# Softmax totals of attention for two groups of heads in one pass of the matmul array, and their inverses spread by transfers inside the chip

## The chip, the cores and the metric

The kernel runs on one core of one Trainium2 chip. A core has a matmul engine (TensorE, PE in the profile), a vector engine (VectorE, DVE), a scalar engine for activation functions (ScalarE, ACT), GpSimd (POOL) and SyncE (SP), from which most transfers are issued. Each engine works through its own queue in order, and waits on semaphores for what others make. Working data is in SBUF (128 partitions); matmuls write to PSUM, whose banks hold 512 float32 values on each of 128 partitions. The metric is device time in microseconds (us), from the start to the end of one execution; lower is better.

## The reference, cut to what matters

Four layers follow each other on x of shape (8, 512, 32, 32): an attention layer with an inner iteration (layer 0), a second attention (layer 1), a filtered leaky ReLU (layer 2), and convolutions with weights mixed per sample (layer 3). The change is in layer 0 alone:

```python
h = group_norm(x, gn_scale, gn_bias)
qkv = einsum('oc,bchw->bohw', qkv_w, h) + qkv_b       # 512 channels each for q, k, v
q, k, v = to_heads(q), to_heads(k), to_heads(v)       # 8 heads of 64, S = 1024 positions
attn = softmax(einsum('bnsd,bntd->bnst', q, k) * 64 ** -0.5, axis=-1)
h = einsum('bnst,bntd->bnsd', attn, v)
for _ in range(3):                                    # h is (B, S, 512) here
    h = h + 0.1 * tanh(einsum('bsc,oc->bso', h, inl_w) + inl_b)
x = x + einsum('oc,bchw->bohw', proj_w, h) + proj_b
```

The softmax's division is done last: the kernel multiplies exponentials by v, adds up the exponentials over the keys, and multiplies the product by one over that total.

## The kernel before, in words

All of it is float32. The eight samples ("batches", `b`) go through layers 0 to 2 one after another; layer 3 follows for all. The attention of layer 0 is in `layer0`. A batch has eight *groups* `g`, each one (oc, sh): oc is one of four pairs of heads (128 channels, a head on each 64 partitions) and sh one of two halves of 512 query positions. Groups 0 to 3 are the first half of the positions, 4 to 7 the second. A group has eight *steps*, one for each 128 keys, so a batch has 64 steps.

In each step `i` the loop records, in this order, `scores(i)`, `weighted(i - 2)` and whatever closes an earlier group:

- `scores` (L827) multiplies k by q in four matmuls of 64x64 tiles (two heads, two halves of the keys) that sit on the four quarters of the array; ScalarE takes the exponential of both banks in one instruction (L846); VectorE adds the result to the group's running sum `acc` (L850, L852, and L854 at the eighth step, which also records a sum for a later test of overflow). The exponentials have six buffers.
- `weighted` (L868) multiplies the exponentials by v, again four 64x64 tiles, into two banks `av` of the group. At the eighth step ScalarE copies one bank to `part` (L875) and VectorE adds the other to it (L876), which gives the group's columns of the output `hf`. Even groups take their two banks from one pool of PSUM, odd ones from another.
- `closing(g, at)` stands `at` steps after the step in which the sum of group g can be used. At 0, `totalled` adds up `acc` over the 128 partitions with a matrix of ones: two matmuls (L881) of 128 rows and 64 columns, one for each head, into the group's first `av` bank, so that every one of a head's 64 partitions gets the same total. VectorE takes the reciprocal of 512 columns in two instructions of 256 (L889), at 0 and 1; at 2 it multiplies `hf` by it (L894); at 5 ScalarE reads it once more for the overflow test (L898).

The order on TensorE, VectorE and ScalarE in this stage is the order in which the program records it (`tc.manual_schedule`). Elsewhere, and on SP and GpSimd, a scheduler orders the work and puts in the waits. The last group's closing stands inside the first product of the inner iteration (`within=last_total`, matmuls at L552), together with the sums of quarters of `hf` that this product needs (`T_hf`, L513).

Buffers: `big_tile` gives one of seven SBUF buffers of 16 KB per partition (x, q, k, v, hf, `T_hf` and others take turns in them); `tmp(..., HALF)` one of four of 2 KB (for `part` and `inv`); `sums` one of two of 4 KB (for `acc`). A new tile takes a free buffer, and its first write waits until that buffer's last reader is done. `x = load_x(b)` loads the batch's input again for the projection's sum; on SP's queue the load of the next query weights (L461) stands behind it. `layer2_constants` builds the filter matrices of layer 2 during batch 0, in a big buffer that GpSimd writes first.

Each matmul instruction leaves two records of matmul and two of weight load in the profile: L827 has 4096 records for 8 batches of 64 steps of four matmuls.

Of the kernel before, what the change touches and what calls it, by code (L numbers as in the profile page):

```python
# [17 lines left out]
P = 128  # L18
B, C, H, W = 8, 512, 32, 32
S = H * W  # L20
CC = C // P
SC = S // P
HALF = 512
NH = 8
HD = C // NH
# [12 lines left out]
WE = NE * WX  # L38
EARLY = B - 1
PARTS = ("A11", "A12", "-A22", "S1", "S2", "S3", "S4")  # L40


BOUND = 1e20
# [11 lines left out]
def tile_sequence(ctx: ExitStack, tc: tile.TileContext, a: dict, out: bass.AP, shifted: bool):  # L55
    nc = tc.nc
# [11 lines left out]
    def big_tile(name, shape):  # L68
        return big.tile(shape, F32, tag="big", name=name)
# [5 lines left out]
    def tmp(name, n=HALF):  # L75
        if n == HALF:
            return work.tile([P, n], F32, tag="half", name=name, bufs=4)
        return work.tile([P, n], F32, tag="tmp", name=name, bufs=6)

    def sums(name):  # L80
        return work.tile([P, S], F32, tag="sums", name=name, bufs=2)
# [26 lines left out]
    ones = const.tile([P, P], F32, name="ones")  # L108
# [453 lines left out]
    def all_of(gen):  # L562
        for _ in gen:
            pass
# [232 lines left out]
    def layer0(b, q, k, v, w):  # L797
        hf = big_tile(f"hf_{b}", [P, CC, S])
        rows = [slice(HD * r, HD * r + HD) for r in range(2)]
        shifts = None  # L800
        if shifted:
            shifts = big_tile(f"shifts_{b}", [P, CC, S])
            for oc in range(CC):
                for r in range(2):
                    row_shifts(
                        f"{b}_{oc}_{r}", [q[rows[r], oc, :]] * 2,
                        [k[rows[r], oc, ts(h, HALF)] for h in range(2)],
                        [shifts[HD * r : HD * r + 1, oc, :]],
                    )

        groups = [(oc, sh) for sh in range(2) for oc in range(CC)]
        exps, accs, avs, copies = {}, {}, {}, {}

        def scores(t):
            g, jc = divmod(t, SC)
            oc, sh = groups[g]
            apart = t == 1
            if apart:  # L820
                ps = [bank(ps_tp, f"scores_{b}_{t}_{r}") for r in range(2)]
            else:
                pair = ps_sc.tile([P, S], F32, tag="scores", name=f"scores_{b}_{t}")
                ps = [pair[:, ts(r, HALF)] for r in range(2)]
            for r in range(2):
                for c in range(2):
                    nc.tensor.matmul(  # L827
                        ps[r][rows[c]],
                        k[rows[r], oc, jc * P + c * HD : jc * P + c * HD + HD],
                        q[rows[r], oc, ts(sh, HALF)],  # L830
                        start=True, stop=(shifts is None),
                    )
            if shifts is not None:
                for r in range(2):
                    for c in range(2):
                        nc.tensor.matmul(
                            ps[r][rows[c]], ones[HD * r : HD * r + 1, 0:HD],
                            shifts[HD * r : HD * r + 1, oc, ts(sh, HALF)],
                            start=False, stop=True,
                        )  # L840
            e = tmp(f"e_{b}_{t}", S)
            if apart:
                for r in range(2):
                    nc.scalar.activation(e[:, ts(r, HALF)], ps[r], AF.Exp, scale=HD ** -0.5)
            else:
                nc.scalar.activation(e, pair, AF.Exp, scale=HD ** -0.5)  # L846
            exps[t] = e
            if jc == 1:
                accs[g] = sums(f"acc_{b}_{g}")
                nc.vector.tensor_add(accs[g], exps[t - 1], e)  # L850
            elif 1 < jc < SC - 1:
                nc.vector.tensor_add(accs[g], accs[g], e)  # L852
            elif jc == SC - 1:
                nc.vector.scalar_tensor_tensor(  # L854
                    accs[g], accs[g], 1.0, e, ALU.mult, ALU.add,
                    accum_out=seen_sums[:, b, g : g + 1],
                )

        def weighted(t):
            g, jc = divmod(t, SC)  # L860
            oc, sh = groups[g]
            e = exps.pop(t)
            if jc == 0:
                pool = (ps_mm, ps_tp)[g % 2]
                avs[g] = [bank(pool, f"av_{b}_{g}_{r}") for r in range(2)]
            for r in range(2):
                for c in range(2):
                    nc.tensor.matmul(  # L868
                        avs[g][r][rows[c]], v[rows[r], jc, ts(2 * oc + c, HD)],
                        e[rows[r], ts(c, HALF)],  # L870
                        start=(jc == 0), stop=(jc == SC - 1),
                    )
            if jc == SC - 1:
                part = tmp(f"part_{b}_{g}", HALF)
                nc.scalar.copy(part, avs[g][0])  # L875
                nc.vector.tensor_add(hf[:, oc, ts(sh, HALF)], avs[g][1], part)  # L876

        def totalled(g):
            acc, ps = accs.pop(g), avs.pop(g)[0]
            for r in range(2):  # L880
                nc.tensor.matmul(  # L881
                    ps[rows[r]], ones[:, 0:HD], acc[:, ts(r, HALF)], start=True, stop=True
                )
            totals[g] = ps
            copies[g] = tmp(f"inv_{b}_{g}", HALF)

        def inverse(g, part):
            at = ts(part, QR)
            nc.vector.reciprocal(copies[g][:, at], totals[g][:, at])  # L889

        def scaled(g):
            oc, sh = groups[g]
            dst = hf[:, oc, ts(sh, HALF)]
            nc.vector.tensor_mul(dst, dst, copies[g])  # L894

        def copied(g):
            inv = copies.pop(g)
            nc.scalar.activation(  # L898
                inv, inv, AF.Copy, accum_out=seen_sums[:, b, NG + g : NG + g + 1]
            )  # L900

        def closing(g, at):

            if at == 0:
                totalled(g)
                inverse(g, 0)
            elif at == 1:
                inverse(g, 1)
            elif at == 2:
                scaled(g)  # L910
            elif at == 5:
                copied(g)

        lag, steps, last_g = 2, len(groups) * SC, len(groups) - 1
        totals = {}
        engines = mybir.EngineType
        with tc.manual_schedule(engines={engines.PE, engines.DVE, engines.Activation}):
            for i in range(steps + lag):
                if i < steps:
                    scores(i)  # L920
                if i >= lag:
                    weighted(i - lag)
                g, at = divmod(i - lag - SC - 1, SC)
                if 0 <= g < last_g:
                    closing(g, at)
            t_hf = sum_tiles(f"hf_{b}_0")
            name = f"inl_{b}_0"

            def last_total():
                quarter_sum(t_hf, hf, 0, (0, 1))  # L930
                for at in range(3):
                    closing(last_g, at)
                quarter_sum(t_hf, hf, 1, (0, 1))
                quarter_sum(t_hf, hf, 0, (2, 3))
                quarter_sum(t_hf, hf, 1, (2, 3))

            inner = product(
                name, w["inl"], hf, t_hf, inner_step(name, hf), within=last_total
            )
            for _ in range(2):  # L940
                next(inner)
            copied(last_g)

        x = load_x(b)
        operators = layer2_constants() if b == 0 else iter(())
        next(operators, None)
        all_of(inner)
        for it in (1, 2):
            t = quarter_sums(f"hf_{b}_{it}", hf)
            name = f"inl_{b}_{it}"  # L950
            parts = product(name, w["inl"], hf, t, inner_step(name, hf))
            for i, _ in enumerate(parts):
                for _ in range(2 if i < 4 else 0):
                    next(operators, None)
        all_of(operators)
        if b + 1 < B:
            w["q"] = weight("q", b + 1)
        else:
            load_experts()
        t = quarter_sums(f"hf_{b}_3", hf)  # L960
        all_of(product(f"proj_{b}", w["proj"], hf, t, residual(f"proj_{b}", x)))
        if b + 1 < B:
            w["k"] = weight("k", b + 1)
        else:
            load_experts()
        return x
# [716 lines left out]
```

## Time and profile before

| | us |
|---|---|
| three runs | 3649.09, 3649.24, 3654.0 |
| median | 3649.24 |
| the profiled execution, whole | 3648.9 |
| its span, from the first to the last instruction | 3647.0 |
| attention of layer 0, first scores to last totals, each batch | 120.13 |
| totals L881, 256 records: busy | 69.0 |
| reciprocals L889, 128: busy, mean | 223.1, 1.748 |
| scalings L894, 64: busy, mean | 43.5, 0.680 |
| reads for the overflow test L898, 64: busy, mean | 39.8, 0.622 |

How to read the profile: *busy* is the time in which at least one instruction of a group ran, and a share is a part of the span. [...]the distance between starts shows what one costs. The timeline merges neighbouring instructions of one kind: x8 are eight records. The chain of waits follows the work that ended last back to what released it. A row of transfers gives their number, size, and the median time from issue to landing; a row of waits names who waited for whom, in total, how often, and the longest.

The groups of instructions of the stage, by line (operation, output and input, shapes, number | busy us, mean ns | idle before, and what ended it):

```profile
L846 ACT ACTIVATE e<-scores 128x1024 f32<-128x1024 f32 x504 | 516.6, 1025 | 434.4 <-PE scores L827 379.3
L827 PE MATMUL scores<-q,k 64*64 64x512 f32 x4096 | 531.9, 592 | 0.0
L868 PE MATMUL av<-e,v 64*64 64x512 f32 x4096 | 528.7, 589 | 0.0
L852 DVE TENSOR_TENSOR acc<-acc,e 128x1024 f32<-128x1024 f32 x320 | 389.3, 1217 | 37.4 <-ACT e L846 35.4
L889 DVE RECIPROCAL inv<-av 128x256 f32<-128x256 f32 x128 | 223.1, 1748 | 2.1 <-PE av L881 2.1
```

### The profile page before, as it was taken

How to read it: one execution, taken by the hardware profiler on the slowest of the kernel's cores; microseconds unless marked ns; L12 is line 12 of the kernel's file. 1: busy time of each engine (PE TensorE's matmuls, PEld its weight loads, DVE VectorE, ACT ScalarE, POOL GpSimd, SP SyncE). 2: the span in 40 equal slices, each digit the busy share in tenths (PEclk: the TensorE clock that was granted, in tenths of full speed). 3: DMA queues.
4: the chain of work that ended last, by engine and by line, in shares of the span. 5: the costliest groups of instructions: out<-in, count | busy, mean ns of one | idle time of the engine just before them, and what ended most of it. 6: DMA issues, size and time to landing. Idle time of an engine off the chain costs nothing.

```text
span 3647.0 us, 47655 instructions
## 1 busy us (share of the span) xinstructions
PE 3572.2 (98%) x19445; PEld 1751.4 (48%) x19445; DVE 2406.2 (66%) x3201; ACT 1329.7 (36%) x1772; POOL 102.0 (3%) x139
## 2 busy tenths in 40 slices
PE   8999999999999999999999999999999999999799
PEld 4346543474435643474435743465434744355243
DVE  4887568765777558765687658774687657765434
ACT  0632345223542246223452236323452235422343
POOL 4100000000000000000000000000000000001100
PEclk9999999999999999999999999999999999999999
DMA  5102440116101450015301351024401261015872
GB/s 200 50 1 84 130 162 1 45 65 198 69 1 64 133 179 1 32 53 170 122 1 64 97 174 42 1 84 130 162 1 46 66 201 64 1 43 190 311 272 108
DMA packets 139813, 348.24 MB, mean 95 GB/s; under 512 B 14720, under 2 KB 89488, under 8 KB 132800
## 3 DMA queue, kind: packets, MB, share of 16 engines
q1 hardware_dynamic: 135120, 325.96, 26.0%
q0 software_dynamic: 4320, 18.87, 1.4%
q8 instruction: 155, 2.54, 0.3%
q14 instruction: 74, 0.61, 0.1%
q10 hardware_dynamic: 144, 0.26, 0.0%
HBM read 226.55 MB, written 118.49 MB: 95 GB/s over the span
## 4 chain that ended last, share of the span: by engine, by line
PE 94%; DMA 2%; issue 1%; ACT 1%; DVE 1%; POOL 0%; SPq 0%; POOLq 0%; ACTq 0%; DVEq 0%
PE scores L827 12%; PE av L868 12%; PE inl_X L552 7%; PE inl_A L552 5%; PE av_X L1129 5%; PE inl_Y L552 5%; PE av_A L1129 3%; PE av_Y L1129 3%; PE v_X L552 3%; PE c L1497 2%; PE proj_X L552 2%; PE v_X L607 2%; PE k_X L607 2%; PE v_Y L552 2%; PE av L881 2%; PE q_X L607 2%
## 5 line engine op out<-in xcount | busy, mean ns | idle before, releaser
L846 ACT ACTIVATE e<-scores 128x1024 f32<-128x1024 f32 x504 | 516.6, 1025 | 434.4 <-PE scores L827 379.3
L827 PE MATMUL scores<-q,k 64*64 64x512 f32 x4096 | 531.9, 592 | 0.0
L868 PE MATMUL av<-e,v 64*64 64x512 f32 x4096 | 528.7, 589 | 0.0
L852 DVE TENSOR_TENSOR acc<-acc,e 128x1024 f32<-128x1024 f32 x320 | 389.3, 1217 | 37.4 <-ACT e L846 35.4
L868 PEld LDWEIGHTS av<-e,v 64*64 64x64 f32 x4096 | 156.6, 133 | 282.8 <-issue 276.8
L827 PEld LDWEIGHTS scores<-q,k 64*64 64x64 f32 x4096 | 150.4, 133 | 295.5 <-issue 220.8
L552 PE MATMUL inl_X<-T_hf,w_inl 128*128 128x512 f32 x576 | 261.6, 592 | 0.0
L1195 DVE TENSOR_TENSOR fine<-up,fine 128x1024 f32<-128x1024 f32 x128 | 150.8, 1220 | 118.8 <-ACT fine L1194 116.5
L889 DVE RECIPROCAL inv<-av 128x256 f32<-128x256 f32 x128 | 223.1, 1748 | 2.1 <-PE av L881 2.1
L692 ACT ACTIVATE inl_U<-inl_U,inl_b 128x512 f32<-128x512 f32 x96 | 66.8, 719 | 304.4 <-DVE inl_U L707 304.4
L552 PEld LDWEIGHTS inl_X<-T_hf,w_inl 128*128 128x128 f32 x576 | 108.8, 190 | 137.9 <-issue 111.7
L552 PE MATMUL inl_A<-hf,w_inl 128*128 128x512 f32 x384 | 174.6, 597 | 0.0
L1194 ACT ACTIVATE fine<-up 128x1024 f32<-128x1024 f32 x128 | 124.1, 1022 | 134.1 <-PE up L1188 121.1
L850 DVE TENSOR_TENSOR acc<-e,e 128x1024 f32<-128x1024 f32 x64 | 79.3, 1240 | 111.3 <-ACT e L846 92.3
L703 DVE TENSOR_TENSOR inl_U<-inl_X,inl_P 128x512 f32<-128x512 f32 x96 | 61.8, 685 | 109.9 <-PE inl_X L552 109.9
L1129 PE MATMUL av_A<-v,eT 128*128 128x256 f32 x512 | 122.6, 383 | 0.0
L552 PEld LDWEIGHTS inl_A<-hf,w_inl 128*128 128x128 f32 x384 | 71.5, 190 | 96.8 <-issue 86.3
L1129 PE MATMUL av_X<-v,eT 128*128 128x256 f32 x512 | 114.0, 381 | 0.0
L1016 ACT ACTIVATE eT<-scores 128x512 f32<-128x512 f32 x128 | 66.1, 602 | 115.4 <-PE scores L379 115.4
L1129 PEld LDWEIGHTS av_X<-v,eT 128*128 128x128 f32 x512 | 96.6, 190 | 19.3 <-DVE av_U L1103 6.5
L1166 ACT COPY wide<-wide 128x1024 f32<-128x1024 f32 x62 | 59.8, 1015 | 122.4 <-PE wide L1158 122.4
L1036 POOL TENSOR_TENSOR seen<-seen,acc 128x512 f32<-128x512 f32 x16 | 20.3, 1269 | 3006.6 <-DVE acc L1028 3006.0
(377 smaller groups left out, 5562.2 us busy)
## 6 DMA issues: line engine op xcount, KB each, us to landing
x<-in_x_dram SPq DMA_DIRECT2D x64, 512.0 KB, 9.3
across_u<-wide SPq DMA_DIRECT2D x128, 256.0 KB, 3.7
turned<-across_u SPq DMA_DIRECT2D x64, 512.0 KB, 5.9
back_u<-sent SPq DMA_DIRECT2D x256, 128.0 KB, 2.3
back<-back_u SPq DMA_DIRECT2D x32, 1024.0 KB, 7.6
w_v<-stored_u_v SPq DMA_DIRECT2D x14, 1792.0 KB, 7.4
out_dram<-z SPq DMA_DIRECT2D x31, 512.0 KB, 2.8
spill_u<-z SPq DMA_DIRECT2D x28, 512.0 KB, 5.9
```

The source lines that it names most:

```text
L552: nc.tensor.matmul(dst, lhs, rhs, start=(opens and s == 0 and cc == 0), stop=(cc == 1 and s == rows), skip_group_check=True,)
L607: nc.tensor.matmul(dst, lhs, rhs, start=(what in opens and s == 0 and cc == 0), stop=(cc == 1 and s == rows), skip_group_check=True,)
L827: nc.tensor.matmul(ps[r][rows[c]], k[rows[r], oc, jc * P + c * HD : jc * P + c * HD + HD], q[rows[r], oc, ts(sh, HALF)], start=True, stop= ...
L846: nc.scalar.activation(e, pair, AF.Exp, scale=HD ** -0.5)
L850: nc.vector.tensor_add(accs[g], exps[t - 1], e)
L852: nc.vector.tensor_add(accs[g], accs[g], e)
L868: nc.tensor.matmul(avs[g][r][rows[c]], v[rows[r], jc, ts(2 * oc + c, HD)], e[rows[r], ts(c, HALF)], start=(jc == 0), stop=(jc == SC - 1),)
L881: nc.tensor.matmul(ps[rows[r]], ones[:, 0:HD], acc[:, ts(r, HALF)], start=True, stop=True)
L889: nc.vector.reciprocal(copies[g][:, at], totals[g][:, at])
L1129: nc.tensor.matmul(ps[:, ts(s, QR)], left[:, j, at : at + P], right[:, j, :], start=(what in ("P1", "U2", "C22") and s == 0 and j == 0), s ...
L1194: nc.scalar.mul(t, ps, 0.2)
L1195: nc.vector.tensor_max(t, ps, t)
```

## The change

Groups 0 to 5 of each batch are closed in three pairs (`PAIRS = 3`), groups 6 and 7 as before. The sums of a pair lie together in a big buffer. When the second group of a pair has its sum, `totalled_pair` puts four totals (two groups, two heads each) into one bank with four matmuls of 128 rows and 32 columns, each on its own quarter of the array's columns. Two reciprocals of 128x256 serve both groups. Each total then stands on 32 partitions only, while its head has 64; so `widened` copies each 32-partition piece twice, by transfers from SBUF to SBUF of 64 KB each, eight per pair, into one buffer for each group (`wide_inv`, of the four of 2 KB). The groups' scalings stand nine and ten steps after the totals, the read for the overflow test eleven.

```diff
-        exps, accs, avs, copies = {}, {}, {}, {}
+        exps, accs, avs, copies, wide_inv = {}, {}, {}, {}, {}
...
             if jc == 1:
-                accs[g] = sums(f"acc_{b}_{g}")
+                if g >= 2 * PAIRS:
+                    accs[g] = sums(f"acc_{b}_{g}")
+                elif g % 2 == 0:
+                    both = big_tile(f"accs_{b}_{g}", [P, 2, S])
+                    accs[g], accs[g + 1] = both[:, 0, :], both[:, 1, :]
                 nc.vector.tensor_add(accs[g], exps[t - 1], e)
...
+        def totalled_pair(g):
+            ps = avs.pop(g)[0]
+            del avs[g - 1]
+            for r in range(2):
+                for j, which in enumerate((g - 1, g)):
+                    part = slice(HD * j + W * r, HD * j + W * r + W)
+                    nc.tensor.matmul(
+                        ps[part], ones[:, 0:W], accs[which][:, ts(r, HALF)], start=True, stop=True
+                    )
+            del accs[g - 1], accs[g]
+            totals[g] = ps
+            copies[g] = tmp(f"inv_{b}_{g}", HALF)
+
+        def widened(g):
+            for j, which in enumerate((g - 1, g)):
+                t = wide_inv[which] = tmp(f"wide_inv_{b}_{which}", HALF)
+                for r in range(2):
+                    src = copies[g][HD * j + W * r : HD * j + W * r + W, :]
+                    for at in (HD * r, HD * r + W):
+                        nc.sync.dma_start(t[at : at + W, :], src)
+
+        def scaled_by(g):
+            oc, sh = groups[g]
+            dst = hf[:, oc, ts(sh, HALF)]
+            nc.vector.tensor_mul(dst, dst, wide_inv.pop(g))
+
+        def closing_pair(g, at):
+
+            if at == 0:
+                totalled_pair(g)
+                inverse(g, 0)
+            elif at == 1:
+                inverse(g, 1)
+                widened(g)
+            elif at in (9, 10):
+                scaled_by(g - 10 + at)
+            elif at == 11:
+                copied(g)
...
-                g, at = divmod(i - lag - SC - 1, SC)
-                if 0 <= g < last_g:
-                    closing(g, at)
+                done = i - lag - SC - 1
+                for g in range(1, 2 * PAIRS, 2):
+                    closing_pair(g, done - g * SC)
+                for g in range(2 * PAIRS, last_g):
+                    closing(g, done - g * SC)
```

HD is 64, W is 32, HALF is 512, S is 1024, P is 128, SC is 8.

## The prediction

> **What bounds the kernel now.** I read the page first, then the stage of one batch's attention by windows, then the timeline inside it. The page:
>
> ```profile
> span 3647.0 us, 47655 instructions
> PE 3572.2 (98%) x19445; PEld 1751.4 (48%) x19445; DVE 2406.2 (66%) x3201; ACT 1329.7 (36%) x1772; POOL 102.0 (3%) x139
> PE 94%; DMA 2%; issue 1%; ACT 1%; DVE 1%; POOL 0%; SPq 0%; POOLq 0%; ACTq 0%; DVEq 0%
> ```
>
> TensorE carries 94% of the chain of work that ended last, so an edit counts by the TensorE time that it takes out, unless another engine becomes late. The windows of batch 1, attention first:
>
> ```profile
> core 0: us, PE busy (x) PEld busy (x) DVE busy (x) ACT busy (x) POOL busy (x), PEclk, DMA share, GB/s
> 509.80:630.00 120.20, 120.20 (x1059) 40.47 (x1058) 99.61 (x95) 73.59 (x87) 0.00 (x0) 1.00 0.09 34
> ```
>
> TensorE is never idle there, VectorE has 20.6 us to spare, and the transfers use 9%. So attention is TensorE's, and its length is a count of matmul sets. The timeline around the first totals (start, length, engine, line):
>
> ```profile
> 104.21 1.04 PE L868 MATMUL av<-e,v 64*64 64x512 f32 x8
> ...
> 107.64 1.04 PE L868 MATMUL av<-e,v 64*64 64x512 f32 x8
> ...
> 108.61 1.08 PE L881 MATMUL av<-acc,ones 128*64 128x512 f32 x4
> ...
> 109.62 1.09 PE L827 MATMUL scores<-q,k 64*64 64x512 f32 x8
> 110.09 1.75 DVE L889 RECIPROCAL inv<-av 128x256 f32<-128x256 f32 x1
> ...
> 110.53 1.04 PE L868 MATMUL av<-e,v 64*64 64x512 f32 x8
> ```
>
> An instruction leaves two records (x8 is a set of four 64x64 tiles).[...] Four sets from 104.21 to 107.64 take 3.43 us, 0.857 each. From the last set before the totals to the second one after them are 110.53-107.64 = 2.89 us, of which two plain sets are 1.715. So one insertion of totals costs 1.17 us: its own set and the change of tiling before and after. Check: 128 sets of 0.857, seven insertions of 1.17 and some 1.9 for the projection's first two matmuls make 119.8 of the 120.1 us from the first scores (509.84) to the eighth totals (629.97). No other stall is in the stage.
>
> [...]1.17 against 0.857 is 0.31 us for two changes. It also shows four such tiles at once, in the mixing of the last experts:
>
> ```profile
> 3446.87 1.06 PE L339 MATMUL mix_last<-last_experts,blend_last 128*32 128x512 f32 x8
> ...
> 3447.86 1.55 PE L1497 MATMUL c<-spread,weights 128*128 128x512 f32 x3
> ```
>
> Eight records, four tiles of 128 rows and 32 columns with four different moving operands, hold TensorE 0.99 us to the next set's start; the two tiles of L881 hold it 109.62-108.61 = 1.01.[...]
>
> **The change, part by part.**
>
> *Totals (the gain).* In each of 8 batches groups 0 to 5 had six insertions and now have three. An insertion with four tiles I take at 1.17-0.02 = 1.15 by L339's 0.99, plus 0.01 for two more tiles of 7 ns each: 1.16. Per pair 2x1.17-1.16 = 1.18 us, times 24 is 28.3 us. Bounds of the new insertion: 1.12 (all weight loads shorter) to 1.30 (two more loads of 64x32 weights, about 0.1 each by the trace's records, end to end, not beside each other): gains of 29.3 to 24.9.
>
> *Reciprocals.* 24 pairs drop two of 1.75 us each, 84 us of VectorE. It isn't on the path in this stage, so 0. VectorE's load per pair becomes 14 additions of about 1.22, two of 0.68 for the outputs, two scalings of 0.68 and 3.5 of reciprocals, 23.3 us of the pair's 16x1.715+1.16 = 28.6.
>
> *Copies with a sum (L898).* 24 fewer of 0.62+0.19 on ScalarE, which is busy 73.6 of 120: 0. The one that is left stands six steps later and waits for all eight transfers, with the exponentials queued behind it.
>
> *Transfers.* Eight per pair, 64 KB each, on SP's queue, after the second reciprocal. Rows of before that bound them:
>
> ```profile
> back_u<-sent SPq DMA_DIRECT2D x256, 128.0 KB, 2.3
> SPq L461 <- PE inl_Y L552: 1329.6, 7, 190.8
> ```
>
> Issuing such a 32-partition transfer takes SP about 0.47 us (two in 0.91 in the timeline), landing 2.3. With T0 the start of the totals, the second reciprocal (at 112.97 in before) ends at T0+6.1 (114.72-108.61); the first four are issued by T0+8.0 and land by T0+10.3, the others by T0+12.2. The first scaling stands nine steps after the totals: seven steps (12.0 us) after where L894 stood, whose additions free it at about T0+6, so it is due at T0+18. Slack 7.7 and 7.5 us; cost 0.[...] no run shows SBUF to SBUF of this size. The scaling waits in VectorE's queue with the next additions behind it; six exponential buffers give six steps (10.3 us) less the 2.2 from exponential to addition, so 8 us more before TensorE feels it.
>
> *SP's order.* In the changed program all 24 transfers of a batch stand ahead of its x load, and that ahead of the query weights' load, whose wait is the 190.8 us above; nothing of the transfers is caught behind it. The x load moves from the start of attention to after the third pair, at about 611 for batch 1 (its totals at 601, then 6.1 and eight issues), lands by 625 (9.3 us each), and x is first needed at 710.5 (L738). Cost 0. No other instruction off attention moves on any engine.
>
> *Buffers.* Sums of pairs take three of the seven big buffers. Batch 0's filter constants get the third one's, so POOL writes them after the third totals (about 181, the sixth group's 183.1 of before less two savings, instead of 99.3); with the constants' loads of 6.6 us they are there by 191, and VectorE reads them first at 209.8. Nothing else is in POOL's queue until 335. Cost 0. Outputs' scaled buffers (four): a pair holds three, the fourth serves the copies of L875.
>
> *End of attention.* The two scalings of groups 4 and 5 now fall between group 6's reciprocals, 1.2 us more for VectorE where it is full. Redone op by op from 619.84, L876 of the last group starts at 629.85 instead of 628.78, and the last reciprocals 0.75 us later. Who waits:
>
> ```profile
> 635.83 0.69 DVE L513 TENSOR_TENSOR T_hf<-hf,T_hf 128x512 f32<-128x512 f32 x1
> 636.23 3.60 PE L552 MATMUL inl_X<-T_hf,w_inl 128*128 128x512 f32 x8
> ...
> 640.05 1.28 DVE L703 TENSOR_TENSOR inl_U<-inl_X,inl_P 128x512 f32<-128x512 f32 x2
> ```
>
> The second half of the first inl_X starts at 637.95 and needs what is ready at 636.52; the next one at 642.24 needs L703's first at 640.73. 1.4 and 1.5 us of slack against 0.75: cost 0, up to 0.75x8 = 6 us if my count of VectorE is short by twice.
>
> Sum: 28.3 us. The profiled execution took 3648.9 us (span 3647.0), 0.3 under the median 3649.24; 3648.9-28.3 = 3620.6, and against the median 3621.
>
> **Rivals.**
>
> 1. *VectorE's tail takes part back.* For: its queue is full at the end of attention. Against: the slack above, and 4.5 us idle before L703 soon after. 28.3-6 gives 3627.
>
> 2. *The tiles don't run at once* (the change then doesn't do what it says). For: the four operands come from two buffers through the same rows. Two at a time make the set 2x0.857 and the insertion 2.02: 24x0.32 = 8 us, 3641. One at a time, 3.43 for the set and 3.74 for the insertion, cost 24x1.40 = 34 us: 3683, slower. It decides from an insertion of 2.34 on. Against: L339.
>
> 3. *Transfers late.* A landing over 2.3+7.7+8 = 18 us stalls TensorE through the exponentials; at 19.2 the gain is gone, at 21 the time is some 3691. For: one back_u transfer needed 14.0 us. Against: that was beside others; here the queues are all but empty.
>
> 4. *No difference*: the sets' time reappears as waits on ScalarE or VectorE. Both have over 20 us of spare time in the stage. 3648.
>
> **How the numbers follow.** Full gain 0.86; rival 1, 0.07; rival 2, 0.03 (0.02 of it two at a time); rival 3, 0.02; rival 4, 0.02. The likeliest gives 3621. Its bounds (24.9 to 29.3) reach 3620 to 3624; with part of rival 1 and the spread of medians, 3617 to 3627. About 0.2% (7.3 us) is what a measurement can tell from no change: faster is full gain, rival 1 (22 us) and half-parallel tiles, 0.95; same 0.02; slower 0.03.
>
> **What would show it.** 128x32 totals as x8, three in a batch, about 0.99 us to the next start; attention from the first scores to the last totals 116.6 instead of 120.1; two groups 28.6 apart; no TensorE idle on VectorE around the first inl_X; transfers landed 7 us before their scalings. I am wrong if the set's next start is 1.7 or more later, if TensorE waits on exponentials within a pair, or if time comes or goes outside attention.

## The result, and the profile after

| | before | after |
|---|---|---|
| median of six runs each | 3652.91 us (3649.09 to 3656.84) | 3623.48 us (3620.95 to 3628.34) |
| ratio of after to before, with its 95% interval | | 0.9923 (0.9911 to 0.9934) |
| profiled execution, whole | 3648.9 us | 3623.17 us |
| its span | 3647.0 us | 3621.4 us |
| attention of layer 0, first scores to last totals, each batch | 120.13 us | 116.58 us |
| from the last totals of the last batch to the end | 501.9 us | 505.2 us |

The kernel became faster by 29.4 us in the medians, and by 25.6 us in the spans of the two profiled executions. The page of after begins so:

```profile
span 3621.4 us, 47909 instructions
...
PE 3547.8 (98%) x19445; PEld 1749.8 (48%) x19445; DVE 2332.5 (64%) x3153; ACT 1316.4 (36%) x1724; POOL 101.6 (3%) x139
...
PE 94%; DMA 2%; DVE 1%; ACT 1%; issue 1%; SPq 0%; POOL 0%; ACTq 0%; POOLq 0%; DVEq 0%
```

TensorE has the same 19445 records: 24 times two sets of two tiles became one set of four. Its busy time fell by 24.4 us, VectorE's by 73.7 (2406.2 to 2332.5), and TensorE still carries 94% of the chain. The windows of attention in batch 1 of after (the columns are named in the first line; x counts records):

```profile
core 0: us, PE busy (x) PEld busy (x) DVE busy (x) ACT busy (x) POOL busy (x), PEclk, DMA share, GB/s
506.26:622.84 116.58, 116.58 (x1057) 40.01 (x1056) 89.58 (x88) 71.89 (x81) 0.00 (x0) 1.00 0.15 49
```

TensorE is as full as before in a stage that is 3.55 us shorter. The timeline of after round the first totals of that batch (start, length, engine, line; for the transfers, from the first issue to the end of the eighth):

```profile
538.07 1.04 PE L875 MATMUL av<-e,v 64*64 64x512 f32 x8
539.04 1.07 PE L927 MATMUL av<-accs,ones 128*32 128x512 f32 x8
540.03 1.09 PE L830 MATMUL scores<-q,k 64*64 64x512 f32 x8
540.94 0.61 PE L875 MATMUL av<-e,v 64*64 64x512 f32 x4
...
543.39 1.75 DVE L896 RECIPROCAL inv<-av 128x256 f32<-128x256 f32 x1
...
545.17 4.98 SPq L940 DMA_DIRECT2D wide_inv<-inv  x8
...
557.12 0.68 DVE L945 TENSOR_TENSOR hf<-hf,wide_inv 128x512 f32<-128x512 f32 x1
...
558.86 0.68 DVE L945 TENSOR_TENSOR hf<-hf,wide_inv 128x512 f32<-128x512 f32 x1
```

The printed lengths of neighbours overlap (538.07+1.04 is 539.11, and the totals start at 539.04), so costs are counted from start to start. The four totals hold TensorE from 539.04 to 540.03, 0.99 us. From the last set before them to the second set after them are 540.94-538.07 = 2.87 us; less the two plain sets, 1.715, the insertion costs 1.16 us, like one of two tiles (1.17). The first scaling starts 18.1 us after the totals and no idle time stands beside it. None of the 48 scalings of this execution waited for a transfer.

Where the 25.6 us between the two spans come from:

| part | us |
|---|---|
| attention, 8 x 3.55 | +28.4 |
| the first loads, until the first scores of batch 0 (89.56 and 88.72) | +0.8 |
| batch 0 after its attention | -0.8 |
| a pause in one batch of before, not explained (distance to the next 419.57, others 419.10) | +0.5 |
| from the last totals to the end | -3.3 |

The gain is in the place that was named, in full. Two entries have the other sign, and the experiments go after both.

**Batch 0.** From one batch's first scores to the next, before needs 420.27 us in batch 0 and mostly 419.10 later (1.17 more), after 417.54 and 415.55 (1.99 more). The timeline of after behind batch 0's attention (the bracket is idle time before the instruction, and what ended it):

```profile
211.56 3.83 PE L555 MATMUL inl_X<-T_hf,w_inl 128*128 128x512 f32 x8
215.23 2.74 PE L555 MATMUL inl_Y<-T_hf,w_inl 128*128 128x512 f32 x6
218.31 3.67 PE L555 MATMUL inl_X<-T_hf,w_inl 128*128 128x512 f32 x8 [0.34 <-DVE inl_U L706]
```

And the same place before:

```profile
215.96 3.60 PE L552 MATMUL inl_X<-T_hf,w_inl 128*128 128x512 f32 x8
219.39 2.74 PE L552 MATMUL inl_Y<-T_hf,w_inl 128*128 128x512 f32 x6
...
220.38 1.28 DVE L703 TENSOR_TENSOR inl_U<-inl_X,inl_P 128x512 f32<-128x512 f32 x2
...
221.97 3.60 PE L552 MATMUL inl_X<-T_hf,w_inl 128*128 128x512 f32 x8
```

From start to start the first product takes 3.67 instead of 3.43 us, and the one after it 3.08 instead of 2.58: 0.74 us lost, with VectorE named as what was late. VectorE's own timeline of after shows what stands in its queue there:

```profile
206.32 0.18 DVE L166 TENSOR_SCALAR setup<-setup 64x32 f32<-64x32 f32 x1
206.51 0.56 DVE L173 TENSOR_TENSOR setup<-setup 128x384 f32<-128x384 f32 x1
...
210.87 0.11 DVE L165 TENSOR_SCALAR setup<-setup 128x12 f32<-128x12 f32 x1
...
212.20 0.55 DVE L176 TENSOR_TENSOR setup<-setup 128x384 f32<-128x384 f32 x1
...
216.88 1.28 DVE L706 TENSOR_TENSOR inl_U<-inl_X,inl_P 128x512 f32<-128x512 f32 x2
```

Four instructions of the filter's setup (1.4 us), which only batch 0 has, use up most of the slack that the other batches keep. L706 (before it is L703) starts 5.32 us after the first inl_X (216.88-211.56), against 4.42 before (220.38-215.96): 0.9 us later, and here that is too late. The next inl_X waits for both of its instructions: they end at 216.88+1.28 = 218.16, and TensorE goes on at 218.31. Before, they ended at 221.66, only 0.3 us ahead of the inl_X that needs them.

**The end.** From the last totals on, the two kernels' TensorE starts agree to 0.01 us for the first 196 us. Of the 3.3 us, 2.7 arise between the first `up` product and the first `c<-spread` product, where the experts' weights are mixed (102.11 and 104.80), and 0.6 behind it. The windows before, from the second half of the last totals to the first `up`, and from there to the first `c<-spread`:

```profile
3145.55:3342.01 196.46, 194.16 (x722) 116.81 (x718) 130.38 (x215) 42.30 (x68) 3.56 (x4) 1.00 0.15 52
3342.01:3444.12 102.11, 74.56 (x447) 23.47 (x447) 42.38 (x59) 37.20 (x56) 18.95 (x35) 0.95 0.97 348
```

And after:

```profile
3116.64:3313.09 196.45, 194.16 (x722) 116.81 (x718) 131.09 (x216) 42.30 (x68) 3.56 (x4) 1.00 0.16 52
3313.09:3417.89 104.80, 78.90 (x446) 25.62 (x447) 42.46 (x59) 37.68 (x56) 18.95 (x35) 0.90 0.95 342
```

This stage is the transfers': they are busy 97% and 95% of it and TensorE three quarters. 102.11x348 and 104.80x342 are 35.5 and 35.8 MB, the same within a per cent; they moved a little slower.

### The profile page after: what moved, and what is told of

Its sections match the earlier page's. It is cut to its first block, busy times and chain, and to the rows that moved or that the text cites. A ratio compares the mean times of both kernels' runs of the same rounds, so it can differ in the third digit from the quotient of the medians.

```text
span 3621.4 us, 47909 instructions
## 1 busy us (share of the span) xinstructions
PE 3547.8 (98%) x19445; PEld 1749.8 (48%) x19445; DVE 2332.5 (64%) x3153; ACT 1316.4 (36%) x1724; POOL 101.6 (3%) x139
## 4 chain that ended last, share of the span: by engine, by line
PE 94%; DMA 2%; DVE 1%; ACT 1%; issue 1%; SPq 0%; POOL 0%; ACTq 0%; POOLq 0%; DVEq 0%
PE scores L830 12%; PE av L875 12%; PE inl_X L555 7%; PE av_X L1177 5%; PE inl_Y L555 4%; PE inl_A L555 4%; PE av_A L1177 3%; PE av_Y L1177 3%; PE v_X L555 3%; PE c L1545 2%; PE proj_X L555 2%; PE v_X L610 2%; PE k_X L610 2%; PE v_Y L555 2%; PE v_A L555 2%; PE q_X L610 2%
## 5 line engine op out<-in xcount | busy, mean ns | idle before, releaser
L859 DVE TENSOR_TENSOR accs<-accs,e 128x1024 f32<-128x1024 f32 x240 | 294.2, 1226 | 50.8 <-ACT e L849 46.7
L896 DVE RECIPROCAL inv<-av 128x256 f32<-128x256 f32 x80 | 138.9, 1745 | 0.0
L706 DVE TENSOR_TENSOR inl_U<-inl_X,inl_P 128x512 f32<-128x512 f32 x96 | 61.8, 685 | 106.4 <-PE inl_X L555 106.4
L857 DVE TENSOR_TENSOR accs<-e,e 128x1024 f32<-128x1024 f32 x48 | 59.6, 1242 | 100.2 <-ACT e L849 81.2
L859 DVE TENSOR_TENSOR acc<-acc,e 128x1024 f32<-128x1024 f32 x80 | 96.8, 1210 | 8.4 <-ACT e L849 7.6
```

## The experiments

The theory: an insertion costs a set and 0.31 us on top (1.17-0.857 before), whatever the number of tiles; that the 0.31 goes to the two changes of tiling is the author's reading of the trace. So three insertions fewer per batch are the whole gain; the saved reciprocals and reads are worth next to nothing, and the transfers are covered. Rivals: part of the gain comes from relieving VectorE and ScalarE; or the transfers cost something; or what is lost at the end belongs to the change. Ratios are to the kernel before, with 95% intervals; "attention" is from first scores to last totals.

### One pair instead of three

```diff
-PAIRS = 3
+PAIRS = 1
```

> PAIRS = 1: only groups 0 and 1 of each batch share their totals, the other six are closed singly. Theory (what counts is the TensorE time of the insertions, one fewer per pair): a third of the gain, 8 x 1.18 = 9.5 us under the kernel before, ratio 0.9974; attention from the first scores to the last totals 118.95 us in each batch. Rival (part of the gain comes from VectorE's relief, which shows only when its queue is eased throughout): clearly less than a third, under 7 us, or attention over 119.3.

Measured: ratio 0.9971 (0.9958 to 0.9983), median 3642.1 us against 3652.15; attention 118.95 us in every batch, 120.13-1.18. A pair is worth one insertion, 1.18 us, and three of them add up to the 3.55.

### The saved sets put back, everything else as changed

Two totals of the old form are computed once more for the first group of each pair, at their old place, and not used.

```diff
+            if at == -SC:
+                for r in range(2):
+                    nc.tensor.matmul(
+                        avs[g - 1][0][rows[r]], ones[:, 0:HD], accs[g - 1][:, ts(r, HALF)],
+                        start=True, stop=True,
+                    )
```

> The changed kernel, and in addition the first group of each pair still gets its own set of two 128x64 totals at its old place, which nobody reads. Reciprocals, transfers and scalings are those of the changed kernel. Theory: 24 insertions of 1.17 come back, the whole gain goes: within 1 us of the kernel before (ratio 1.000), attention 120.1 us. Rival (84 us fewer of VectorE and 19 fewer of ScalarE are worth something by themselves, or the transfers cost something): the time differs from before by more than 5 us, or attention by more than 0.3 us.

Measured: ratio 0.9997 (0.9988 to 1.0006); attention 120.09 us. With seven insertions again, the gain is gone, though this kernel has six reciprocals and three reads on ScalarE fewer in a batch than before, and all 192 transfers. So the gain is TensorE's insertions, and all the rest of the change together is worth 0.04 us a batch in attention. Batch 0 takes 1.99 us more than the others here too (421.06 against 419.07), so that loss hangs on the pairs' closing and not on the totals.

### The saved reciprocals put back

Each pair's two reciprocals are done a second time, two and three steps after the totals, into a buffer that nothing reads.

```diff
+            elif at in (2, 3):
+                if at == 2:
+                    copies[g, "again"] = sums(f"again_{b}_{g}")
+                part = ts(at - 2, QR)
+                nc.vector.reciprocal(copies[g, "again"][:, part], totals[g][:, part])
```

> The changed kernel, and VectorE takes the two reciprocals of each pair a second time, two and three steps after the totals, into a buffer that nobody reads: 24 x 3.5 = 84 us of VectorE come back, TensorE's instructions stay. Theory: VectorE's load per pair is 23.3 + 3.5 = 26.8 of 28.6 us, so no change: attention 116.6, time within 2 us of the changed kernel. Rival (VectorE's load counts): attention over 117.5, several us in all.

Measured: ratio 0.9925 (0.9908 to 0.9941); attention 116.80 us in seven batches and 117.15 in one. 84 us of VectorE's work (48 of 1.75) cost 0.22 us in a batch, all of it between the last `weighted` matmul and the totals of group 7 (2.65 instead of 2.43 us), where TensorE waits for VectorE's sum. In all that is 7x0.22+0.57 = 2.1 us, the price of the reciprocals at these places and beside the late scalings. It is no part of the 28.4: in the run above the sets alone took the gain away.

### Two sets of two tiles in one place

The pair's totals keep the old form, 128x64, but both groups' sets stand next to each other. There are four reciprocals, no transfers, scalings at 2 and 4 and reads for the overflow test at 5 and 6.

```diff
-                totalled_pair(g)
-                inverse(g, 0)
...
+                for which, ps in zip((g - 1, g), avs.pop(g)):
+                    for r in range(2):
+                        nc.tensor.matmul(
+                            ps[rows[r]], ones[:, 0:HD], accs[which][:, ts(r, HALF)],
+                            start=True, stop=True,
+                        )
...
+            if at in (2, 4):
+                scaled(g - 1 if at == 2 else g)
+            elif at in (5, 6):
+                copied(g - 6 + at)
```

> The pair is closed in one place, but with 128x64 totals as before: two sets of two tiles, one for each group, into the two banks of the second group; four reciprocals, no transfers, scalings two and four steps after. So one change of tiling to and fro is saved per pair, and no set. Theory: an insertion of 1.17 + 0.857 = 2.03 us in place of 2.34, 24 x 0.31 = 7.5 us under before (ratio 0.998), attention 119.2; the remaining 21 us of the gain are the halved sets. Rival (the change of tiling is what costs, a set more adds little): nearer to the changed kernel than to before.

Measured: ratio 1.0026 (1.0018 to 1.0033), slower, attention 121.2 us. The insertion itself came out as expected. From its timeline:

```profile
542.90 1.04 PE L875 MATMUL av<-e,v 64*64 64x512 f32 x8
...
543.87 1.94 PE L953 MATMUL av<-accs,ones 128*64 128x512 f32 x8
...
546.65 1.04 PE L875 MATMUL av<-e,v 64*64 64x512 f32 x8
```

546.65-542.90-1.715 = 2.03 us for two sets in one place, against 1.16 for the set of four tiles. The second set adds 2.03-1.17 = 0.86 us, as much as a plain set (0.857), so the 0.31 is paid once for both. The loss is elsewhere, 15 us later:

```profile
557.93 0.69 DVE L901 TENSOR_TENSOR hf<-hf,inv 128x512 f32<-128x512 f32 x1
...
558.65 0.63 ACT L905 ACTIVATE inv<-inv 128x512 f32<-128x512 f32 x1 [1.61 <-DVE hf L901]
...
559.28 1.92 ACT L849 ACTIVATE e<-scores 128x1024 f32<-128x1024 f32 x2
...
560.34 1.09 PE L830 MATMUL scores<-q,k 64*64 64x512 f32 x8 [0.56 <-ACT e L849]
```

With four reciprocals VectorE reaches the second scaling only at 557.93. ScalarE's read of that inverse stands in ScalarE's queue two steps after the scaling's place, waits 1.61 us for VectorE, and the exponentials wait behind it until TensorE runs dry. That was a reading of the timeline, so the next run tests it.

### The same with the reads later

```diff
-            elif at in (5, 6):
-                copied(g - 6 + at)
+            elif at in (10, 11):
+                copied(g - 11 + at)
```

> As two sets in one place, with the reads for the overflow test ten and eleven steps after the totals instead of five and six; the four reciprocals, the scalings and the two sets of totals stay. Theory A, that ScalarE's read stood in its queue waiting for VectorE's late second scaling with the exponentials behind it: attention of layer 0 takes 119.2 us in a batch (120.13 less three times 0.31 for the two changes of tiling saved), the ratio to the kernel before is about 0.998. Theory B, that VectorE itself is late with the running sums after four reciprocals in a row, so that exponentials find no buffer: attention stays at about 121.2 us and the ratio at 1.002 to 1.003.

Measured: ratio 0.999 (0.9983 to 0.9997); attention 119.55 us in every batch. Theory A holds for 1.65 of the 2.0 us; of the other 0.35, the second and third pair's totals start 0.07 later each, as do group 6's, and group 7's 0.15. That VectorE is a little late with four reciprocals fits this, but was not tested. This version tells what four tiles at once with half the reciprocals are worth beyond putting two groups' totals in one place: 119.55-116.58 = 3.0 of the 3.55 us, of which the sets are 3x(2.03-1.16) = 2.6.

### The scalings at 5 and 6

```diff
-            elif at in (9, 10):
-                scaled_by(g - 10 + at)
+            elif at in (5, 6):
+                scaled_by(g - 6 + at)
```

> The changed kernel with the two scalings of a pair five and six steps after the totals in place of nine and ten. The transfers have landed by then (10.9 and 13.1 us after the totals; the scalings are due at about 11.2 and 12.9). It takes the two scalings of groups 4 and 5 out of the reciprocals of group 6. Theory (the 0.74 us that batch 0 loses before its second inl_X comes from VectorE's full queue at the end of attention): that wait goes, in batch 0 alone, attention stays at 116.58; the time is 0.7 us lower, which the median can't tell. Rival (the wait in batch 0 comes from the filter constants, which are written later): it stays.

Measured: ratio 0.9922 (0.9905 to 0.9938), attention 116.58 us, and batch 0 takes 416.73 us, 1.18 more than the others, as before the change. So the 0.8 us lost in batch 0 come from the two late scalings of the third pair among group 6's reciprocals, and not from the filter constants. It is worth 0.8 us in 3623, which the medians can't tell.

### The scalings at 2 and 3, ahead of the landings

```diff
-            elif at in (9, 10):
-                scaled_by(g - 10 + at)
+            elif at in (2, 3):
+                scaled_by(g - 3 + at)
```

> The changed kernel with the scalings two and three steps after the totals, where the single groups have theirs. The transfers now come too late: VectorE waits some 3.5 us for the first and 1 us for the second. Theory (six exponential buffers give TensorE 8 us of cover, and VectorE makes up 4.5 us within the 5.3 that it has free in a pair): VectorE shows the waits, TensorE none, attention 116.6, same time. Rival (the transfers are on the path as soon as VectorE waits for them): 24 x 4.5 = 108 us at most, attention up to 130.

Measured: ratio 0.9951 (0.9934 to 0.9967), slower than the change by some 9 us; attention 117.4 to 118.6 us. The scalings now wait, which measures the landings. From VectorE's timeline, with the totals at 541.47:

```profile
551.62 0.69 DVE L945 TENSOR_TENSOR hf<-hf,wide_inv 128x512 f32<-128x512 f32 x1 [2.97 <-DMA wide_inv<-inv]
...
555.18 0.69 DVE L945 TENSOR_TENSOR hf<-hf,wide_inv 128x512 f32<-128x512 f32 x1 [1.74 <-DMA wide_inv<-inv]
```

In this pair the inverses of the first group can be used 10.2 us after the totals and those of the second 13.7 us after; in the 24 pairs it is 10.0 to 11.1 and 12.6 to 13.9. The first and second pair's waits, 4.7 us here and 3.6 to 4.9 in all, cost TensorE nothing. After the third pair it stalls:

```profile
608.86 0.69 DVE L945 TENSOR_TENSOR hf<-hf,wide_inv 128x512 f32<-128x512 f32 x1 [2.96 <-DMA wide_inv<-inv]
...
612.08 0.69 DVE L945 TENSOR_TENSOR hf<-hf,wide_inv 128x512 f32<-128x512 f32 x1 [1.40 <-DMA wide_inv<-inv]
...
614.07 1.08 PE L888 MATMUL av<-acc,ones 128*64 128x512 f32 x4 [0.39 <-DVE acc L861]
...
626.82 1.08 PE L888 MATMUL av<-acc,ones 128*64 128x512 f32 x4 [1.02 <-DVE acc L861]
```

Group 6's totals stall in four of the eight batches, group 7's in all. Group 6's come eight steps after the pair's and not sixteen, and they need VectorE's sum itself, not only a free exponential buffer. The expectation counted the buffers' cover alone.

### The same for the first two pairs only

```diff
-            elif at in (9, 10):
-                scaled_by(g - 10 + at)
+            elif g < 5 and at in (2, 3):
+                scaled_by(g - 3 + at)
+            elif g == 5 and at in (9, 10):
+                scaled_by(g - 10 + at)
```

> Scalings two and three steps after the totals for the first two pairs of a batch, nine and ten steps for the third. Theory A, that VectorE makes up what it loses by waiting for the transfers before the next totals need it, and that only the third pair's lag met totals (those of groups 6 and 7): attention 116.6 us in every batch, ratio 0.992. Theory B, that each early scaling costs TensorE time by itself: two thirds of what three cost, so attention 117.1 to 117.9 us and a ratio of 0.994.

Measured: ratio 0.9917 (0.99 to 0.9933), attention 116.58 us in every batch. Theory A holds: waits of 3.6 to 5.2 us a pair on VectorE cost nothing where the next totals come sixteen steps later. With all three pairs early, totals that come eight steps later stalled at once.

### The scalings at 2 and 3, each transfer issued twice

```diff
                     for at in (HD * r, HD * r + W):
-                        nc.sync.dma_start(t[at : at + W, :], src)
+                        for _ in range(2):
+                            nc.sync.dma_start(t[at : at + W, :], src)
```

with the scalings at 2 and 3 as above.

> As the last, and each transfer is issued twice: SP needs 16 issues of 0.6 us, so the pieces are there 12.9 and 17.7 us after the totals, and VectorE waits about 9 us per pair, more than the 5.3 that it has free. Theory: VectorE falls behind by 3.6 us per pair; TensorE feels it when the lag passes 8 us, so attention grows by a few us per batch (0 to 6), in its second half, through exponentials that wait for their buffers; 0 to 50 us in all. Rival (all waits are hidden): 116.6. Other rival (each wait is paid in full): attention 143.

Measured: ratio 1.0252 (1.0235 to 1.0269), median 3745.24 us against 3651.58, much more than expected; attention 131 to 133 us. The waits of a pair are 6.54 and 3.24 us in the second pair of batch 1, 9.8 in all, and this time TensorE runs out of exponentials:

```profile
593.97 11.10 SPq L941 DMA_DIRECT2D wide_inv<-inv  x16
...
601.51 0.69 DVE L946 TENSOR_TENSOR hf<-hf,wide_inv 128x512 f32<-128x512 f32 x1 [6.54 <-DMA wide_inv<-inv]
...
604.51 1.09 PE L830 MATMUL scores<-q,k 64*64 64x512 f32 x8 [0.43 <-ACT e L849]
...
606.58 0.69 DVE L946 TENSOR_TENSOR hf<-hf,wide_inv 128x512 f32<-128x512 f32 x1 [3.24 <-DMA wide_inv<-inv]
...
609.59 1.98 PE L830 MATMUL scores<-q,k 64*64 64x512 f32 x8 [3.13 <-ACT e L849]
```

9.8 us of waiting made 0.43+3.13 = 3.6 us of idle TensorE, a cover of 6.2 us. In the first pair of that batch 6.80+3.17 us made 1.88, a cover of 8.1. In the eight batches the first pair's cover is 8.1 each time, the second's 5.6 to 6.2. The set that follows the stall is printed with 1.98 us instead of 1.04. The windows show the clock beside it (the last three columns are the granted TensorE clock, the share of the transfers and GB/s):

```profile
605.70:609.11 3.41, 0.76 (x8) 0.00 (x0) 2.53 (x4) 0.60 (x1) 0.00 (x0) 1.00 0.08 19
609.11:612.52 3.41, 2.93 (x16) 1.04 (x20) 3.31 (x4) 2.88 (x5) 0.00 (x0) 0.50 0.00 0
612.52:615.93 3.41, 3.41 (x36) 1.13 (x32) 3.10 (x4) 1.54 (x3) 0.00 (x0) 1.00 0.00 0
```

This stall is paid twice: TensorE is idle for 3.13 us, and then its granted clock is 0.50 from 609.11 on, for 3.41 us. Before group 6's totals the idle time is 6.32 us, and the clock is 0.50 for 6.83 us (639.83 to 646.66).

### The changed kernel, the kernel before and the early version once more

> The changed kernel once more, for a second profile. The first one is 25.6 us under the profile of before where the attention alone gives 28.4; 2.9 us of it stand in the 90 us in which the experts' weights come in (transfers busy 94%). Theory (that stage runs at the rate of the transfers, which differs from one execution to the next): attention 116.58 again in each batch, and the stage's length differs from 90.0 by a us or more. Rival (the change costs 2.9 us there): 90.0 again, and 87.1 in every profile of a kernel without the pairs' buffers and transfers.

Measured for the changed kernel: ratio 0.9921 (0.9905 to 0.9938), median 3623.73 us; its last stages take 505.3 us. Attention is 116.58 us again, and the mixing of the experts' weights moved by 0.9 us, so neither the theory (a us or more) nor the rival (none) holds as written.

> The kernel before once more, for a second profile of its last stages. Theory A, that the length from the last totals of attention to the end varies between executions of one program (the stage that mixes the experts' weights is bound by transfers): it differs from 501.9 us by 1 us or more. Theory B, that it belongs to the program: 501.9 within 0.3, and attention 120.13 either way.

Measured for the kernel before: attention 120.13 us and 501.9 us from the last totals to the end, as theory B has it (3649.95 us in this one execution).

> The kernel with the early scalings of the first two pairs once more, for its last stages. Theory A, that the length of the stage that mixes the experts' weights belongs to the program: from the last totals to the end 502.4 us within 0.9 (as far as the two profiles of the changed kernel and of the kernel before lie apart at most), median 3621. Theory B, that it varies between executions: anywhere from 501.9 to 506.9, and the median as that of the changed kernel, 3623 to 3624. Attention 116.58 in both.

Measured for the early scalings of two pairs: 503.2 us to the end (502.4 the first time), but median 3624.12 us instead of 3621.04, ratio 0.9922 (0.9909 to 0.9936). The stage from the first `up` to the first `c<-spread` takes:

| kernel | us |
|---|---|
| before, two profiles | 102.1, 101.8 |
| changed, two profiles | 104.8, 105.7 |
| scalings at 5 and 6 | 106.8 |
| early scalings of two pairs, two profiles | 102.4, 103.2 |
| one pair | 102.3 |
| sets put back | 104.1 |
| reciprocals put back | 102.9 |
| two sets in one place (no transfers), reads early and late | 102.7, 103.4 |
| scalings at 2 and 3, transfers single and doubled | 102.3, 105.3 |

Two profiles of one program lie within 0.9 us, as theory A has it. The medians of the early scalings moved by 3.1 us between two measurements, as theory B has it, but these were on different chips, and the kernel before moved with them, from 3650.9 to 3652.3. Three programs with all the 192 transfers are at 102.3 to 103.2 here (scalings at 2 and 3, reciprocals put back, early scalings of two pairs), and one without any is at 103.4, so by these single executions neither the transfers nor the shorter attention cause the 3 us by themselves. Nor does TensorE's clock: its mean in this stage is 0.90 in the second profile of before, with 101.8 us, as in the first of the changed kernel, with 104.8. What sets the speed of the transfers in this stage was not tried, and stays open.

Whether a loss comes with the change is open too. The medians differ by 3652.91-3623.48 = 29.4 us, and in the repetition by 3651.58-3623.73 = 27.9, where attention and batch 0 alone give 28.4-0.8 = 27.6. That speaks against a loss, but the interval of the first ratio stands for a gain of 24.1 to 32.5 us, and a loss of 3 us fits into it. The profiled execution of before, at 3648.9, lies 4 us under its median.

No version was faster than the changed kernel by more than the measurements can tell.

## Why the prediction was right

The forecast was the full gain, 3621 us; the six runs' median is 3623.48, inside the range, and 0.9923x3649.24 = 3621.1 us on the footing on which the forecast was made. That it agrees to 0.1 us is chance, as the interval is some 4 us to each side; the attention stage is the better witness.

- *Totals.* An insertion of four tiles was put at 1.16 us and took 1.16 (next start 0.99 us later, as read from the experts' mixing); one of two tiles 1.17. The 0.01 us for two more tiles was added although L339's 0.99 is of four tiles already; it is too small to matter. The gain in attention was put at 28.3 us and was 28.4. One pair alone and the sets put back show that it is this and, within 0.04 us a batch, nothing else.
- *Reciprocals at 0.* Done a second time they cost 0.22 us in most batches, 2.1 in all. Right in kind; the end of attention, where VectorE is full, is the exception.
- *Transfers.* The second reciprocal ends 6.1 us after the totals, as counted. An issue was put at 0.47 us, from two of another kind, and eight take 4.98, 0.62 each. With the scalings early, the first group's inverses could be used after 10.0 to 11.1 us (10.3 was said), the second's after 12.6 to 13.9 (12.2 was said). From issue to landing these transfers took 2.0 us in the median, where 2.3 was put. The slack of the second group's inverses, due 19.8 us after the totals (558.86-539.04), is therefore some 6 to 7 us and not 7.5; the cost 0 stands.
- *The cover behind a late scaling*, "8 us more before TensorE feels it", holds for the first pair only (8.1 us in the run with doubled transfers). It was 5.6 to 6.2 in the second, and after the third some 4: there 2.96+1.40 us of waits made 0.39 us of idle before group 6's totals and more before group 7's, since totals need VectorE's sum and not only a free buffer. At the changed kernel's places this didn't matter, but the third rival's threshold of 18 us for a landing, which rests on the 8 us, was too generous for the second and third pair.
- *End of attention* at 0. VectorE's lateness was put at 0.75 us; it is 0.5 in batch 1 (L706 starts 4.32 us after the first inl_X, L703 before 3.82) and 0.9 in batch 0. In seven batches it costs nothing. The step that failed is the slack, in two ways. The prediction let the second inl_X wait for the first of L703's two instructions only, 1.5 us ahead. It waits for both, as batch 0 shows, and they end at 641.33 for a start at 642.24: 0.9 us. And the slack was read from batch 1 and used for all eight, while batch 0 has four setup instructions in VectorE's queue at that place and only 0.3 us left. The first rival came true for that one batch, at 0.8 us, and so did the sign of it, TensorE idle on VectorE round the first inl_X.
- *SP's order, the x load and the filter's constants* at 0: no wait of TensorE points to them, and the batches after the first keep their time outside attention (415.55-116.58 = 298.97, before 419.10-120.13 = 298.97).
- "If time comes or goes outside attention" was named as a sign against. 3.3 us went behind the last attention in the profiled execution, 2.7 of them in the experts' mixing, a stage not considered. The medians are too wide to say whether they belong to the change.

## What to carry to other kernels

Small products that interrupted a stream of another tiling cost 1.16 us here with four column tiles and 1.17 with two, where a plain set takes 0.857; two sets in one place cost 2.03, so the 0.31 us on top of a set was paid once per interruption. So fill all four quarters before paying, and let transfers undo the layout: with the saved sets put back, all the rest of the change, the 192 transfers among it, was worth 0.04 us a batch in attention. When work is moved later on an engine with spare time, look at the place where that engine is full, in the first pass of the loop too, where setup work can share the queue. The cover of a wait ends at the first consumer that needs the waiting engine's result itself, so count the steps to that one, not only the free buffers (here some 4 us after the third pair, where the first had 8.1).

## What the runs showed of the hardware that was not expected

**After stalls the granted TensorE clock was 0.50, in pieces of 3.41 us and multiples of it.** In the run with doubled transfers the granted clock is 0.50 from 609.11 to 612.52 and from 639.83 to 646.66, pieces of 3.41 and 6.83 us, and the starts are 30.72 us apart, nine times 3.413. In the profile of after it is 0.50 from 3332.17 to 3335.58, from 3352.65 to 3359.47 and from 3397.02 to 3407.26, pieces of 3.41, 6.83 and 10.24 us, with starts 20.48 and 44.37 us apart, six and thirteen times 3.413. The stretch of 3.41 us before a piece was not always empty: the one before 609.11 had 0.76 us of work. After one at 0.50 with 2.20 us of work (639.83 to 643.24) the clock was still 0.50; after the next, with 3.42 us, it was 1.00, as it was after the one from 609.11, with 2.93:

```profile
636.42:639.83 3.41, 0.00 (x0) 0.00 (x0) 0.77 (x2) 0.00 (x0) 0.00 (x0) 1.00 0.55 133
639.83:643.24 3.41, 2.20 (x8) 0.62 (x12) 3.41 (x5) 0.00 (x0) 0.00 (x0) 0.50 1.02 402
643.24:646.66 3.42, 3.42 (x20) 1.00 (x18) 3.32 (x3) 1.02 (x1) 0.00 (x0) 0.50 0.37 149
646.66:650.07 3.41, 3.41 (x36) 1.10 (x33) 3.41 (x4) 1.73 (x2) 0.00 (x0) 1.00 0.00 0
```

The profiles of before and after, cut into steps of 3.413 us that meet these pieces, from 30 us on, show the same (work is TensorE's busy time as printed, with modelled ends). At full clock, six stretches were followed by half clock, with 0.00 to 1.26 us of work, and the stretches with 1.49 us or more by full clock. At half clock, the clock stayed at 0.50 after stretches with up to 2.61 us and was 1.00 after those with 3.05 us or more. These are figures of two executions; where the limits lie was not shown.

**A transfer of 64 KB inside the chip** took 2.0 us from issue to landing in the median, 1.9 at least and 3.8 at most, of the 192 in the changed kernel; issuing one took SP 0.59 us in the median.
